# One frequency per 128x32 matmul tile in the mixing stage of a two-layer spectral kernel

## Chip, core and metric

The kernel runs on one core of a Trainium2 chip. The time is the device time of one execution in microseconds; a median of three runs is given for the kernel before.

A core has four engines that matter here: PE (TensorE: matmuls, with a weight load of its own, PEld), DVE (VectorE), ACT (ScalarE) and POOL (GpSimd). SP only issues DMAs. Matmuls write PSUM, which DVE and ACT copy out to SBUF; DMAs go between SBUF and the HBM.

## What is computed

The input is 16 images (B) of 16 channels (C), 256 x 256. Layer 0 is a 3x3 circular convolution of the group-normalized input, layer 1 a Laplace layer; each adds its result to its input. In layer 1 every frequency of the transformed image has a 16 x 16 complex matrix of its own:

```python
    x = x + _L0_conv_ref(_gn(x), L0_conv_weight)
    x = x + _L1_conv_ref(_gn(x), ...)
    # in _L1_conv_ref:
    alpha = jnp.fft.fft2(x, axes=(-2, -1))
    A = 1.0 / (omega1[:, None, None, None] - weights_pole1[None])
    Bm = 1.0 / (omega2[:, None, None, None] - weights_pole2[None])
    S = jnp.einsum('ikpq,oikp,xikq->oxik', weights_residue, A, Bm)
    output_residue1 = jnp.einsum('biox,oxik->bkox', alpha, S)
    x1 = jnp.fft.ifft2(output_residue1, s=(Ny, Nx), axes=(-2, -1)).real
```

A second term, x2, comes from the poles alone (exponentials in y and x). The change touches `output_residue1`, the product over the channels i at each frequency, which the kernel calls mixing.

## The kernel before

There are three stages, one after the other. The first convolves, normalizes and makes the forward transform; it leaves the spectrum in the HBM array `aD` (128 rows of x frequencies, 32 rows of real and imaginary channels, 256 y frequencies by 16 images). The second, the mixing, reads `aD` and writes `yD`. The third reads `yD`, transforms back, adds the transient and the input and writes the output.

The mixing stage (lines 994 to 1284) works through 32 rounds of `g` (L1242). A round handles four x frequencies (`s`): the 128 rows of a matmul are 4 x 32, real and imaginary channels. A round has four places `n` (L1250), and a place 64 of the 256 y frequencies. For each place:

- `sums` (L1036) makes on PE the weights of the next round, in PSUM banks `ps_s`, for two places at a time (at even n). Four banks hold two places.
- `spread` (L1060) copies them into the weights' tile `sg`, half by ACT (L1066) and half by DVE as a shuffle (L1069), in two steps (`odds`), which stand before the first and the second mix of the place.
- `mix` (L1132) multiplies: weights from `sg`, the moving operand from `abd[jq]`, in which each s has its own rows and all others are zero, so that the four x frequencies come out in separate columns. Four PSUM banks `ps_mix` take turns.
- the copy (L1265) brings `ps_mix` to the tile `yt`, on ACT or DVE by `m`; `late` gives one more copy to DVE in the steps in which ACT has Exp or Sin to do.
- `store` (L1153) writes `yt` to `yD`, and `load` (L1115) fetches the spectrum of the next round into the same `abd[jq]`; so that load waits for the last mix of the place. Places 0 and 1 share one tile (`pair`) and are loaded together at n = 1, before that place's store; at the other places the store comes first. All these DMAs are issued by SP, in the order in which they stand.
- steps of `weights` (small DVE and POOL work for a later round) and of `make_exps` (L1182: POOL and ACT work for the third stage) are drawn in, one a place.

Before the change two neighbouring frequencies are taken by one matmul. `sg` holds them side by side (`m e`: channel, then even or odd), so that weights of 64 columns serve both; the moving operand has 128 columns, both frequencies times 4 x 16. Each output of 64 rows by 128 columns has the products of each frequency with each spectrum, and half of them (even with odd) is of no use; the copy takes it along and the store picks the useful rows (`yt[e::2, e]`), in two DMAs. The output's upper and lower 64 rows (`t`) take two matmuls of different frequencies. A place has four mixes of eight such matmuls.

After round 30 `unmix_first` (L1160) puts one row of `yD` right: it reads it into the free `sg` tile, works on it on DVE and writes it back.

In the third stage `load_images` (L1315) fetches the first channel's spectra in pieces, as the stage starts, and `load_quarter` (L1337) fetches a later channel's in four DMAs, each ahead of its use. `combine` on POOL, `along_x` and `along_y` on PE follow. `pitched` (L62) lays out `aD` and `yD` with 256 floats between rows and 1024 at the end of a partition's part.

Of the kernel before, what the change touches and what calls it, by code (L numbers as in the profile page):

```python
# [9 lines left out]
FP = mybir.dt.float32  # L10
# [6 lines left out]
B = 16  # L17
C = 16
N = 256
# [5 lines left out]
def conv_then_laplace_kernel(ctx: ExitStack, tc: tile.TileContext, a: dict, out: bass.AP):  # L25
# [44 lines left out]
        t = dp.tile([P, C, 8 * N + 256], FP, name=f"vD{b}", tag=f"vD{b}")  # L70
        vD.append(t[:, :, 0 : 8 * N].rearrange("p c (b h x) -> p c b h x", b=4, h=2))
    aD = pitched("aD", 2 * C, N * B)
    yD = pitched("yD", 4 * C, N * B // 2, 2, 4)
    cD = dp.tile([P, 4, 8, N], FP, name="cD", tag="cD")
    hD = dp.tile([7, 2, 16, C * C * 4], FP, name="hD", tag="hD")
    eD = [dp.tile([n, P, C, 2, P], FP, name=f"eD{n}", tag=f"eD{n}") for n in (2, 1)]
# [570 lines left out]
    def chain(*gens):  # L647
        for gen in gens:
            yield from gen
# [100 lines left out]
    def pool(stage, name, bufs=1, **kw):  # L750
        return stage.enter_context(tc.tile_pool(name=name, bufs=bufs, reuse_waits="tile", **kw))
# [242 lines left out]
    ptab.close()  # L994


    yp = pool(p2, "yt", 3)
    g0 = pool(p2, "sg0")
    a0 = pool(p2, "abd0")
    wp = pool(p2, "w", 2)  # L1000
# [7 lines left out]
    pm = pool(p2, "p_mix", 4, space=PSUM)  # L1008

    def new_sg(g):  # L1010
        return (g0, g1)[g % 2].tile([P, P, 2 * C, 2], FP, name="sg", tag="sg")

# [37 lines left out]
    swap = [p ^ 4 for p in range(32)]  # L1052

    def couples(z):
        return z.rearrange("p q (n e) -> p n q e", e=2)

    def columns_of(to, k):
        return to[:, :, k : k + 2] if len(to.shape) == 4 else to[:, k : k + 2]

    def spread(n, *pairs, odds=(0, 1)):  # L1060

# [9 lines left out]
    def first_sums():  # L1071

        nc.gpsimd.memset(pair, 0.0)
        wt, w128 = (at_once(steps) for steps in first_weights)
        load(0, 1)
        nc.gpsimd.memset(abd[2], 0.0)
        load(0, 2)
        nc.sync.dma_start(  # L1080
            out=aD[16:P, 2 * C - 2 : 2 * C], in_=spec[16:P].rearrange("p r f b -> p r (f b)")
        )
        nc.gpsimd.tensor_tensor(accs, proj[:, :, :, :, 0], proj[:, :, :, :, 1], ALU.add)
        sg = new_sg(0)
        other = up["u"].tile([P, 2, 2 * C], FP, name="other", tag="other")
        for h, w in enumerate((wt, w128)):
            for n in range(4):
                fy = slice(P * h, P * h + P)
                ps = sums(n, w)
                spread(  # L1090
                    n,
                    (sg[:, 64 * h : 64 * h + 64], [couples(z[:, :, fy]) for z in ps]),
                    (other[:, 1 - h], [z[:, :, P * (1 - h)] for z in ps]),
                )
        for h in range(2):
            o, d = sg[:, 64 * h, :, 0], other[:, h]
            nc.vector.tensor_tensor(d, d, o, ALU.subtract)
            nc.vector.scalar_tensor_tensor(o, d, fixrow, o, ALU.mult, ALU.add)
        return sg
# [29 lines left out]
                    out=abd[jq][s::4, s].rearrange("r c j b -> r c (j b)"), in_=src[:, :, jq]  # L1129
                )  # L1130

    def mix(n, sg, yt):  # L1132


        ps = pm.tile([P, 4, 2, 4, B], FP, name="ps_mix", tag="ps_mix")
        jq = n // 4
        for j in range(4):
            cc, jj = divmod(4 * (n % 4) + j, 8)
            for t in range(2):
                f = 128 * t + 64 * cc + 16 * jq + 2 * jj  # L1140
                nc.tensor.matmul(  # L1141
                    ps[64 * t : 64 * t + 64, j],
                    lhsT=sg[:, f // 2].rearrange("p m e -> p (m e)"),
                    rhs=abd[jq][:, :, 2 * t + cc, 2 * jj : 2 * jj + 2].rearrange(
                        "p s j b -> p j s b"
                    ),
                    start=True,
                    stop=True,
                )
        j0 = 4 * (n % 4)  # L1150
        return yt[:, :, :, j0 : j0 + 4], ps.rearrange("p j o s b -> p o (s b) j")

    def store(g, jq, yt):  # L1153
        for e in range(2):
            nc.sync.dma_start(
                out=yD[4 * g : 4 * g + 4, :, e, jq].rearrange("s k n -> k s n"),
                in_=yt[e::2, e].rearrange("p (s b) j -> p s (b j)", s=4),
            )

    def unmix_first():  # L1160

        z2 = new_sg(32).rearrange("p (a n) m e -> p a (n m e)", a=4)[:, 0:2]
        z, t = (z2[:, j, 0:1024].rearrange("p (c n) -> p c n", c=4) for j in range(2))
        at = yD[0]
        for c in range(4):
            nc.sync.dma_start(out=z[:, c], in_=at[32 * (c // 2) : 32 * (c // 2) + 32, c % 2])
        yield
        lo, hi = z[:, 0:2], z[:, 2:4]  # L1170
        nc.vector.scalar_tensor_tensor(t[:, 0:2], hi, osgn, lo, ALU.mult, ALU.add)
        nc.vector.scalar_tensor_tensor(t[:, 2:4], lo, nosgn, hi, ALU.mult, ALU.add)
        nc.vector.tensor_scalar(t, t, 0.5, None, ALU.mult)
        t0, z0 = t[:, 0:3:2, 0:256:16], z[:, 0:3:2, 0:256:16]
        nc.vector.tensor_tensor(z0, z0, t0, ALU.subtract)
        nc.vector.scalar_tensor_tensor(t0, z0, first, t0, ALU.mult, ALU.add)
        for c in range(4):
            nc.sync.dma_start(out=at[32 * (c // 2) : 32 * (c // 2) + 32, c % 2], in_=t[:, c])

    def make_exps(which):  # L1182
# [12 lines left out]
        for q in range(8):  # L1195
            th = ep.tile([P, 2, N], FP, name="s_th", tag="s_th")
            rn = ep.tile([P, N], FP, name="s_rn", tag="s_rn")
            tmp = ep.tile([P, N], FP, name="s_tmp", tag="s_tmp")
            ex = ep.tile([P, 2, N], FP, name="s_ex", tag="s_ex")
            for j in range(2):  # L1200
                i = 2 * q + j
                nc.gpsimd.tensor_scalar(th[:, j], t, pim[:, i : i + 1], None, ALU.mult)
            magic = 1.5 * 2.0**23
            c1 = 6.28125
            c2 = float(np.float32(1.93500518798828125e-3))
            c3 = 2 * np.pi - c1 - c2
            for j in range(2):
                z = th[:, j]
                nc.gpsimd.tensor_scalar(rn, z, 1.0 / (2 * PI), turns, ALU.mult, ALU.add)
                nc.gpsimd.tensor_scalar(rn, rn, magic, magic, ALU.add, ALU.subtract)  # L1210
                for c in (c1, c2, c3):
                    nc.gpsimd.tensor_scalar(tmp, rn, float(c), None, ALU.mult)
                    nc.gpsimd.tensor_tensor(z, z, tmp, ALU.subtract)
                yield
            nc.gpsimd.tensor_scalar(th, th, most, least, ALU.min, ALU.max)
            for j in range(2):
                i = 2 * q + j
                nc.scalar.activation(ex[:, j], t, AF.Exp, scale=pl[:, i, 0:1])
            yield True
            yield  # L1220
            nc.scalar.activation(th, th, AF.Sin, bias=phase)
            yield True
            nc.gpsimd.tensor_tensor(th, th, ex, ALU.mult)
            for op, eo in ((ALU.add, 0), (ALU.subtract, 1)):
                nc.gpsimd.tensor_tensor(
                    ex[:, :, eo * P : eo * P + P], th[:, :, 0:P], th[:, :, N - 1 : P - 1 : -1], op
                )
            yield
            for o in range(2 - which):
                nc.sync.dma_start(  # L1230
                    out=eD[which][o, :, 2 * q : 2 * q + 2].rearrange("p i e t -> p i (e t)"),
                    in_=ex,
                )
            yield
# [3 lines left out]
    ahead, wt = first_sums(), None  # L1238
    o2 = finish_projections()
    unmix = None  # L1240
    exps, late = chain(make_exps(0), make_exps(1)), None
    for g in range(32):  # L1242
        sg, w_now = ahead, wt
        if g == 0:
# [5 lines left out]
        for n in range(4):  # L1250
# [6 lines left out]
            elif sets and n % 2 == 0:  # L1257
                banks = {j: sums(j, w_now) for j in (n, n + 1)}
            evict = [banks[j] for j in sets]
            yt = yp.tile([P, 2, 4 * B, 16], FP, name="yt", tag="yt")  # L1260
            for m in range(4):
                for j, ps in zip(sets, evict) if m < 2 else ():
                    spread(j, (ahead, [couples(z) for z in ps]), odds=(m,))
                o, src = mix(4 * n + m, sg, yt)
                (nc.vector.tensor_copy if m >= (2 if late else 3) else nc.scalar.copy)(o, src)  # L1265
            if n == 1 and g < 31:
                load(g + 1, n)
            store(g, n, yt)
# [6 lines left out]
            if n == 3:  # L1275
                steps = weights(g + 3) if g < 29 else iter(())
            wt = next_step(steps, None) or wt
            late = g and next(exps, None)
        if g == 30:
            unmix = unmix_first()  # L1280
            next(unmix)
# [33 lines left out]
    def load_images(yk, b0, rows, eng):  # L1315

        at = slice(16 * b0, 16 * b0 + 64)
        for r in range(2):
            for h in range(2):
                eng.dma_start(  # L1320
                    out=yk[r][rows, h].rearrange("p c b j -> p c (b j)")[:, :, at],
                    in_=yD[rows, 2 * C * h + C * r].rearrange("p e q n -> p (e q) n")[:, :, at],
                )

    def load_tables(k, eng=nc.gpsimd):
# [11 lines left out]
    def load_quarter(k, n, yk):  # L1337
        r, h = divmod(n, 2)
        nc.sync.dma_start(
            out=yk[r][:, h].rearrange("p c b j -> p (c b j)"),  # L1340
            in_=yD[:, 2 * C * h + C * r + at(k)].rearrange("p e q n -> p (e q n)"),
        )

    def load_v(k, b0):
# [305 lines left out]
```

## Time and profile before

| | |
|---|---|
| median of 3 runs | 2562.41 us (2560.56 to 2570.66) |
| the profiled execution | 2559.74 us, span 2557.7 us |
| mixing stage | about 1206 to 1794 us |
| a round of the mixing stage | 18.05 us |
| DMA in that stage | 0.77 of 16 engines, 248 GB/s |
| third stage | about 1794 to 2557 us |

The page gives for every engine its busy time, as a share of the span and in 40 slices, and then groups of instructions by line, engine, operation and form: `128*64 128x128` is a tile of the array of 128 rows by 64 columns with 128 moving columns, x its count, followed by busy time, mean ns of one, and the idle time ahead of it with what ended it. An fp32 matmul stands there as two weight loads and two matmul records. The other views ask the trace for a stretch of time: busy time of each engine, instructions in order, DMA packets.

### The profile page before, as it was taken

Reading aid. Unit: us, or ns where it says so; the run is one execution under the profiler, and the core shown is the slowest. Engines: PE = TensorE matmul, PEld = TensorE weight load, DVE = VectorE, ACT = ScalarE, POOL = GpSimd, SP = SyncE. Lnnn points to the kernel's source line nnn. Section 1 sums busy time; section 2 is a strip of 40 time slices with the busy share of each in tenths; the row PEclk is TensorE's granted clock in tenths of the full one; section 3 lists DMA queues with packets and bytes.
Section 4 is the critical chain, followed back from the end, with each engine's and each line's share of the span. In section 5 each row is a group of like instructions: output and inputs, shape, how many; then the busy total and the mean of one; then the engine's idle time right before and its main releaser. Section 6 shows DMA issues by size and latency. Waiting matters only on the chain. (4 is left out here: it accounts for less than half of the span.)

```text
span 2557.7 us, 83730 instructions
## 1 busy us (share of the span) xinstructions
PE 2446.8 (96%) x35314; PEld 1895.7 (74%) x35314; DVE 1836.5 (72%) x3771; ACT 1433.9 (56%) x2603; POOL 1255.0 (49%) x1277
## 2 busy tenths in 40 slices
PE   4999999999999999998999999999899999999998
PEld 2454555457777777775899999998688888888887
DVE  7777789848888888887566666665367676666766
ACT  2566666675666666665677767776344434444443
POOL 1333369442333333334376756664655655556553
PEclk9999999999999999999999999999899999999999
DMA  7889878865456456456777777777988888889884
GB/s 272 271 292 300 280 264 292 289 239 201 189 224 247 194 218 247 194 219 216 230 255 248 255 253 246 243 244 247 278 286 292 293 291 283 294 282 306 282 290 167
DMA packets 314070, 653.11 MB, mean 255 GB/s; under 512 B 45238, under 2 KB 160054, under 8 KB 301792
## 3 DMA queue, kind: packets, MB, share of 16 engines
q1 hardware_dynamic: 312720, 644.23, 73.2%
q8 instruction: 278, 4.55, 0.7%
q0 software_dynamic: 928, 3.02, 0.5%
q10 hardware_dynamic: 48, 0.52, 0.2%
q14 instruction: 96, 0.79, 0.1%
HBM read 368.15 MB, written 280.36 MB: 254 GB/s over the span
## 5 line engine op out<-in xcount | busy, mean ns | idle before, releaser
L1362 POOL TENSOR_TENSOR u<-yk 128x512 f32<-128x512 f32 (+1 forms) x268 | 351.7, 1345 | 313.8 <-PE ps_p L1398 243.9
L300 PE MATMUL ps_conv<-xt,wc 32*32 32x512 f32 x12288 | 447.2, 606 | 30.5 <-issue 21.0
L1141 PEld LDWEIGHTS ps_mix<-abd,sg 128*64 128x64 f32 x8192 | 446.8, 137 | 36.7 <-issue 30.0
L1141 PE MATMUL ps_mix<-abd,sg 128*64 128x128 f32 x8192 | 463.4, 274 | 9.2 <-DVE yt L1265 4.9
L300 PEld LDWEIGHTS ps_conv<-xt,wc 32*32 32x32 f32 x12288 | 252.3, 104 | 212.5 <-issue 117.7
L802 ACT ACTIVATE t<-ps_y,vmr 128x384 f32<-128x384 f32 x512 | 296.8, 580 | 156.6 <-PE ps_y L794 156.4
L786 PE MATMUL ps_y<-tabE,vq 128*128 128x256 f32 x1024 | 313.3, 388 | 1.8 <-ACT t L802 1.8
L794 PE MATMUL ps_y<-tabO,vq 128*128 128x256 f32 x1024 | 305.9, 380 | 0.0
L1422 PE MATMUL ps_f<-pt,inv 128*128 128x256 f32 x1008 | 300.5, 380 | 0.0
L1423 PE MATMUL ps_f<-hs,ey 128*128 128x256 f32 x1008 | 299.8, 379 | 0.0
L271 POOL TENSOR_TENSOR pair<-pair,far 128x1024 f32<-128x1024 f32 x64 | 151.7, 2370 | 297.2 <-DVE pair L268 195.5
L1398 PEld LDWEIGHTS ps_p<-inv,u 128*128 128x128 f32 x2048 | 268.6, 193 | 35.3 <-POOL u L1366 11.4
L1398 PE MATMUL ps_p<-inv,u 128*128 128x128 f32 x2048 | 276.2, 278 | 9.9 <-POOL u L1366 9.8
L1426 DVE TENSOR_TENSOR r<-ps_f,q 128x256 f32<-128x256 f32 x256 | 106.9, 418 | 245.0 <-ACT q L1425 224.1
L1265 ACT COPY yt<-ps_mix 128x512 f32<-128x512 f32 x352 | 203.2, 586 | 110.6 <-PE ps_mix L1141 39.4
L1425 ACT COPY q<-ps_f 128x256 f32<-128x256 f32 x256 | 95.4, 372 | 273.9 <-PE ps_f L1423 250.4
L786 PEld LDWEIGHTS ps_y<-tabE,vq 128*128 128x128 f32 x1024 | 189.5, 191 | 78.6 <-ACT q L842 50.3
L1265 DVE COPY yt<-ps_mix 128x512 f32<-128x512 f32 x160 | 108.9, 688 | 180.8 <-PE ps_mix L1141 175.4
L1400 ACT COPY pt<-ps_p 128x512 f32<-128x512 f32 x256 | 151.5, 592 | 137.1 <-PE ps_p L1398 137.1
L666 POOL TENSOR_TENSOR vq<-vf 128x512 f32<-128x512 f32 x63 | 80.1, 1272 | 289.8 <-DVE vf L670 278.8
L1066 ACT ACTIVATE sg<-ps_s,mcol 128x512 f32<-128x512 f32 (+1 forms) x264 | 178.5, 677 | 68.8 <-PE ps_s L1043 30.0
L794 PEld LDWEIGHTS ps_y<-tabO,vq 128*128 128x128 f32 x1024 | 195.5, 191 | 26.8
(243 smaller groups left out, 4037.0 us busy)
## 6 DMA issues: line engine op xcount, KB each, us to landing
xt<-in_x SPq DMA_DIRECT2D x288, 258.0 KB
vD<-pair SPq DMA_DIRECT2D x256, 256.0 KB
yD<-yt SPq DMA_DIRECT2D x256, 256.0 KB
vl<-vD SPq DMA_DIRECT2D x128, 512.0 KB
out_y<-ol SPq DMA_DIRECT2D x128, 512.0 KB
s<-vD SPq DMA_DIRECT2D x124, 512.0 KB
aD<-spec SPq DMA_DIRECT2D x15, 4096.0 KB
yk<-yD SPq DMA_DIRECT2D x60, 1024.0 KB
```

What stands on the lines that cost most here:

```text
L271: nc.gpsimd.tensor_tensor(lo, lo, hi, ALU.subtract)
L300: nc.tensor.matmul(acc[r][32 * c : 32 * c + 32], lhsT=ready[b][0][rows, phase, tap], rhs=halves[b][u // 2][rows, q : q + 5 : 4, 2 - tap : ...
L786: nc.tensor.matmul(ps[:, 0:N], lhsT=vf[:, xo, 0, j], rhs=tabE[:, 0 : i + 2 : i + 1], start=True, stop=False, skip_group_check=True,)
L794: nc.tensor.matmul(ps[:, P : P + N], lhsT=vf[:, xo, 1, j], rhs=tabO[:, i : C + 1 : C - i], start=False, stop=True, skip_group_check=True,)
L802: nc.scalar.activation(t[:, xo, j].rearrange("p l n -> p (l n)"), ps[:, 0:384], AF.Copy, scale=vmr[:, 0, b0 + j, i : i + 1],)
L1066: nc.scalar.activation(columns_of(to, k), src[odd], AF.Copy, scale=nsgn)
L1141: nc.tensor.matmul(ps[64 * t : 64 * t + 64, j], lhsT=sg[:, f // 2].rearrange("p m e -> p (m e)"), rhs=abd[jq][:, :, 2 * t + cc, 2 * jj : 2 ...
L1265: (nc.vector.tensor_copy if m >= (2 if late else 3) else nc.scalar.copy)(o, src)
L1362: nc.gpsimd.tensor_tensor(u[:, :, j].rearrange("p b (c n) -> p c b n", c=8), in0, in1, o)
L1398: nc.tensor.matmul(ps[:, at], lhsT=u[:, n], rhs=tab, start=True, stop=True)
L1422: nc.tensor.matmul(ps[:, e], lhsT=tab, rhs=pt[:, e], start=True, stop=False)
L1423: nc.tensor.matmul(ps[:, e], lhsT=ey[:, e], rhs=hs, start=False, stop=True)
```

## The change

Each mixing matmul takes one frequency. The array is cut into four tiles of 128 rows by 32 columns (`c` = 2t + e), each with the 32 weights of one frequency, and the moving operand is that frequency's 64 columns. Nothing in the output is left over, so a PSUM bank holds eight values of j instead of four, and a place has two mixes (`m` = `cc`) of 8 x 4 matmuls in place of four mixes of 4 x 2. `sg` keeps a frequency's 32 channels in one run; `spread` writes into that order. `yt` is half as large, and there are six of it instead of three. A place's results go out in one DMA over 128 partitions. `yD` has 8 x 16 = 128 rows of 1024 floats (plus 256) instead of 64 of 2048 (plus 256). The flag `late` is gone: the first mix's copy is ACT's, the second's DVE's. In the third stage `load_images` has eight DMAs where it had four, and a quarter's load takes two runs of 1024 floats from each partition instead of one of 2048.

```diff
-    yD = pitched("yD", 4 * C, N * B // 2, 2, 4)
+    yD = pitched("yD", 8 * C, N * B // 4, 1, 4)[:, :, 0]
...
-    yp = pool(p2, "yt", 3)
+    yp = pool(p2, "yt", 6)
...
     def new_sg(g):
-        return (g0, g1)[g % 2].tile([P, P, 2 * C, 2], FP, name="sg", tag="sg")
+        return (g0, g1)[g % 2].tile([P, N, 2 * C], FP, name="sg", tag="sg")
...
     def couples(z):
-        return z.rearrange("p q (n e) -> p n q e", e=2)
+        return z.rearrange("p q n -> p n q")
...
-    def mix(n, sg, yt):
-        ps = pm.tile([P, 4, 2, 4, B], FP, name="ps_mix", tag="ps_mix")
-        jq = n // 4
-        for j in range(4):
-            cc, jj = divmod(4 * (n % 4) + j, 8)
-            for t in range(2):
-                f = 128 * t + 64 * cc + 16 * jq + 2 * jj
+    def mix(n, cc, sg, yt):
+        ps = pm.tile([P, 8, 4, B], FP, name="ps_mix", tag="ps_mix")
+        for j in range(8):
+            for c in range(4):
+                t, e = divmod(c, 2)
                 nc.tensor.matmul(
-                    ps[64 * t : 64 * t + 64, j],
-                    lhsT=sg[:, f // 2].rearrange("p m e -> p (m e)"),
-                    rhs=abd[jq][:, :, 2 * t + cc, 2 * jj : 2 * jj + 2].rearrange(
-                        "p s j b -> p j s b"
-                    ),
+                    ps[32 * c : 32 * c + 32, j],
+                    lhsT=sg[:, 128 * t + 64 * cc + 16 * n + 2 * j + e],
+                    rhs=abd[n][:, :, 2 * t + cc, 2 * j + e],
                     start=True,
                     stop=True,
                 )
-        j0 = 4 * (n % 4)
-        return yt[:, :, :, j0 : j0 + 4], ps.rearrange("p j o s b -> p o (s b) j")
+        return yt[:, :, 8 * cc : 8 * cc + 8], ps.rearrange("p j s b -> p (s b) j")

     def store(g, jq, yt):
-        for e in range(2):
-            nc.sync.dma_start(
-                out=yD[4 * g : 4 * g + 4, :, e, jq].rearrange("s k n -> k s n"),
-                in_=yt[e::2, e].rearrange("p (s b) j -> p s (b j)", s=4),
-            )
+        nc.sync.dma_start(
+            out=yD[4 * g : 4 * g + 4, :, jq].rearrange("s k n -> k s n"),
+            in_=yt.rearrange("p (s b) j -> p s (b j)", s=4),
+        )
...
-            yt = yp.tile([P, 2, 4 * B, 16], FP, name="yt", tag="yt")
-            for m in range(4):
-                for j, ps in zip(sets, evict) if m < 2 else ():
+            yt = yp.tile([P, 4 * B, 16], FP, name="yt", tag="yt")
+            for m in range(2):
+                for j, ps in zip(sets, evict):
                     spread(j, (ahead, [couples(z) for z in ps]), odds=(m,))
-                o, src = mix(4 * n + m, sg, yt)
-                (nc.vector.tensor_copy if m >= (2 if late else 3) else nc.scalar.copy)(o, src)
+                o, src = mix(n, m, sg, yt)
+                (nc.vector.tensor_copy if m else nc.scalar.copy)(o, src)
...
         for r in range(2):
-            for h in range(2):
+            for c in range(4):
+                h, e = divmod(c, 2)
                 eng.dma_start(
-                    out=yk[r][rows, h].rearrange("p c b j -> p c (b j)")[:, :, at],
-                    in_=yD[rows, 2 * C * h + C * r].rearrange("p e q n -> p (e q) n")[:, :, at],
+                    out=yk[r][rows, h, 4 * e : 4 * e + 4].rearrange("p c b j -> p c (b j)")[:, :, at],
+                    in_=yD[rows, 2 * C * c + C * r][:, :, at],
                 )
...
         nc.sync.dma_start(
-            out=yk[r][:, h].rearrange("p c b j -> p (c b j)"),
-            in_=yD[:, 2 * C * h + C * r + at(k)].rearrange("p e q n -> p (e q n)"),
+            out=yk[r][:, h].rearrange("p (e c) b j -> p e (c b j)", e=2),
+            in_=yD[:, 4 * C * h + C * r + at(k) :: 2 * C][:, 0:2].rearrange("p e q n -> p e (q n)"),
         )
```

## The prediction

> **What bounds the kernel now.** I read the page first: the span, the busy shares, the 40 slices. PE is busy 96% of the span, and in every slice but the first, so each stage has to be asked what its PE time is made of.
>
> ```profile
> span 2557.7 us, 83730 instructions
> PE 2446.8 (96%) x35314; PEld 1895.7 (74%) x35314; DVE 1836.5 (72%) x3771; ACT 1433.9 (56%) x2603; POOL 1255.0 (49%) x1277
> ...
> L1141 PEld LDWEIGHTS ps_mix<-abd,sg 128*64 128x64 f32 x8192 | 446.8, 137 | 36.7 <-issue 30.0
> L1141 PE MATMUL ps_mix<-abd,sg 128*64 128x128 f32 x8192 | 463.4, 274 | 9.2 <-DVE yt L1265 4.9
> ...
> L1265 ACT COPY yt<-ps_mix 128x512 f32<-128x512 f32 x352 | 203.2, 586 | 110.6 <-PE ps_mix L1141 39.4
> ...
> L1265 DVE COPY yt<-ps_mix 128x512 f32<-128x512 f32 x160 | 108.9, 688 | 180.8 <-PE ps_mix L1141 175.4
> ```
>
> The copies out of PSUM wait for the mixing matmuls; these wait for next to nothing. The tile view of ps_mix puts the stage at 1206 to 1794 us, 32 rounds of g. Next the table by stretches, with two rounds in mid-stage:
>
> ```profile
> core 0: us, PE busy (x) PEld busy (x) DVE busy (x) ACT busy (x) POOL busy (x), PEclk, DMA share, GB/s
> 1502.88:1520.93 18.05, 18.05 (x387) 16.29 (x385) 10.60 (x28) 11.49 (x20) 5.76 (x7) 1.00 0.81 265
> ...
> 1575.08:1593.13 18.05, 18.05 (x387) 16.29 (x385) 11.39 (x29) 12.64 (x21) 9.93 (x11) 1.00 0.79 249
> ```
>
> A round lasts 18.05 us with PE busy throughout and the others at 10 to 12.6; but the DMA engines are busy 0.8 of it, and they are second in line. The timeline of one half round shows the two parts of PE's work, and the DMA view the cost of packets over 25 rounds (1250 to 1701.25):
>
> ```profile
> 1502.88 1.96 PE L1043 MATMUL ps_s<-ct,w 64*32 64x256 f32 x64
> ...
> 1504.76 7.21 PE L1141 MATMUL ps_mix<-abd,sg 128*64 128x128 f32 x128
> ...
> 1511.90 1.96 PE L1043 MATMUL ps_s<-ct,w 64*32 64x256 f32 x64
> ```
>
> ```profile
> DMA packets 101252, 112.17 MB, mean 249 GB/s; under 512 B 8510, under 2 KB 85670, under 8 KB 101158
> ## 3 DMA queue, kind: packets, MB, share of 16 engines
> q1 hardware_dynamic: 101158, 110.78, 76.1%
> ```
>
> Half a round is 1.88 us of ps_s and 7.14 us of mixing: 128 records (each fp32 matmul leaves two), so 55.8 ns a record. Two 128*64 tiles run side by side, so a tile takes a 128-column record every 111 ns. The DMA: 0.761 x 16 x 451.25 us / 101158 packets = 54 ns a packet of mostly 1 KB; 112.17 MB / 25 = 4.49 MB a round; all queues together hold 77.3% (76.1 + 1.1 + 0.1) of the time, so a round needs 0.773 x 18.05 = 13.95 us of 16 busy engines.
>
> **What the skill says.** "TensorEngine Tiling (Array Packing)", Performance Considerations, promises up to 4x for column tiling, but warns of some 60 cycles a matmul (so do not shrink a dimension that is small already) and of PSUM evacuation as the next bottleneck. "TensorE: Matmul & The Clock Gate", Back-to-back issue gap, gives N/2.4 + 2.5 ns a matmul of N columns, with a floor near 25 ns. The trace agrees with the slope if a record passes each column twice: 2 x 128/2.4 + 2.5 = 109 ns against 111. It does not bear the floor out where several tiles work: 60 records of ps_h on 32*32 tiles took 1.43 us in the chain (24 ns, 256 columns each), and they started about 7 ns apart in a burst and 17 ns later. "DMA: Bandwidth & Descriptors", Rules for kernel authors, advises one 128-partition transfer instead of two halves, since both share the same 16 engines: so I take no bandwidth from the single store.
>
> **The change, part by part.**
> (1) Matmuls. Before, a round issues 128 matmuls = 256 records, 128 columns on two tiles; half of each output is thrown away. After: 8 x 4 x 8 = 256 matmuls = 512 records, 64 columns on four tiles. A 128*32 tile stands in the trace already: psd. Its 16 records take 0.66 us with one of 0.273 us to drain, so (0.66 - 0.273)/15 = 26 ns a record, 103 ns a tile for 128 columns, as on 128*64: narrowing costs nothing and four tiles do run side by side. For 64 columns no row exists. From below, half of it: 2 x 64/2.4 + 2.5 = 56 ns a tile, 14 ns a record. From above, no gain from the halved columns: 26 ns. I take 14, because the slope fits 128 and 256 columns (256: 2 x 256/2.4 + 2.5 = 216; ps_s on eight tiles 1.88 us / 64 x 8 = 235 with its drain). A 32-column weight load (psd's 110 ns against 137) overlaps, as now. PE's round: 512 x 14 = 7.2, plus 2 x 1.88 of ps_s, plus some 0.3 of drains: **11.2 us** (17.2 from above).
> (2) Copies. 16 per round become 8, each still 128x512. ACT loses 11 - 4 = 7 x 0.586 = 4.1 us a round, DVE 5 - 4 = 1 x 0.688 = 0.7. ACT goes to some 8, DVE to some 10.5: not the bound. The flag that moved a copy to DVE in the steps with Exp and Sin goes: ACT's table load and two Exps (1.28 + 2 x 0.50) now stand in front of ACT's copy and of the next sums' eviction. PE's slack under the DMA bound (about 3 us) covers that; without it, 2.3 us twice in seven steps is 1.1 steps x 2.3 = 2.6 us a round.
> (3) Spreads: the same 512 elements, runs of two words rather than four on the write, and a strided PSUM read. Unseen; the mix copies already read PSUM with a long stride at 586 ns, so nothing. From above, 0.1 us on each of 8 a round on either engine, under cover.
> (4) SP. Stores fall from 8 to 4 a round, with twice the rows each. An issue now takes about 0.6 us. Bounds 0.6 to 1.25 us: SP's round is 12 loads x 0.65 + 4 x (0.6 to 1.25) = 10.2 to 12.8 us. The load of abd for the next round stands behind the store of the place before (except at n = 1), which waits for both copies; SP thus stays below the DMA bound, but not by much.
> (5) DMA. Same 1 KB rows, same bytes. More instructions: 512 more a round, two 16 KB blocks, about 0.1 us. So **14.0 us a round** at full share: as PE falls to 11.2, this becomes the bound. The abd tiles are single: their load starts when the last mix of the place has ended. At 1493.96 us the four loads of a pair were issued (2.56 us), and the last packet came some 6.2 us after the first issue; between that point and the next use lie 3.8 of ps_s and 4 x 64 x 14 ns = 1.8 x 2 of mixing, some 7.4 us. Tight, but behind it the stores and other loads keep the queue filled. A full queue is not quite reached: the slices of the page that move most stand at 0.9. I take 0.94: 13.95/0.94 = **14.8 us**, or 303 GB/s, which is the page's best slice (306).
> (6) The last stage. A quarter's load takes 2 x 4 KB rows for one of 8 KB; it is issued more than one unit (11.5 us, a quarter of the 46 us between like entries of the chain) ahead, and PE is 99% busy there (595.62 of 600 us from 1900 on), so nothing. At the seam the first images need 8 POOL DMAs for 4; 4 took 3.71 us, with half the rows each they take less: about +1.9 us (0 to 3.7), on the path, since PE waits there for yk.
>
> **The sum.** Rounds 1 to 29: 29 x (18.05 - 14.8) = 94. Round 0 is held until 1219 us by DMA of the stage before and then by the load of abd[3]: its last mixes shorten by 1.5. Round 30 (15.96 us, no sums) falls to about 14: 2. Round 31 stalls at unmix's read of yD (PE idle about 5 us): 1. Seam: -1.9. Together 97 us. The profiled execution took 2559.7 (span 2557.7): 2463. The median of runs is 2.7 higher: 2465.
>
> **Rivals.** A, the forecast: DMA bound at 0.9 to 1.0 share, rounds of 14.0 to 15.6: 2440 to 2490. B, DMA packets get quicker than the mean shows, since some of their time is other traffic: rounds of 12 to 13.9, near PE's 11.2: 2385 to 2440. For it: a packet's time includes its waiting beside others, and the stage never had to move more than it did. Against: 12.5 us would be 359 GB/s, and no slice of the page passes 306. C, the chain takes over: 64-column records cost up to 26 ns, or ACT's Exp steps and SP's order hold the next pair's load back; rounds of 15.7 to 17.4: 2490 to 2540. D, slower: yD's rows now lie 5 KB apart instead of 9 KB. If that makes the HBM writes dearer, the stage is DMA bound and pays at once: 2048 store packets a round, so 10 ns on each is 1.28 us a round. The DMA needs (18.05 - 14.0)/1.28 x 10 = 32 ns more, 54 to 86, before the round is longer than now; at 100 ns it is 19.9 us, 2562 + 31 x 1.85 = 2620. For it: DMA is second in line already. Against: the 54 ns are a mean over stores of yD and loads of aD, whose rows lie 17 KB apart, and nothing in it points to the stride. E, the change does not do what it says: four tiles queue up one behind the other. Then 56 ns a record and 512 x 56 = 28.7 us a round: about 2970; psd speaks against it.
>
> **Chances.** A 0.58, B 0.12, C 0.15, D 0.08, E 0.03, and 0.04 for a balance at no change. A measurement tells about 0.5% (13 us). Faster 0.85, same 0.04, slower 0.11. The range takes in most of B and nearly all of C: 2415 to 2545.
>
> **What would show it.** Step 1: 16384 records of ps_mix on 128*32, about 14 to 17 ns apart, and a round's PE below 12 us of work. Step 2: 128 copies on each engine. Step 5: a round near 14.8 us with DMA share above 0.9, idle PE before ps_mix put down to abd. It is wrong if PE is again busy through the round, if the share stays near 0.8, or if 1 KB packets cost much over 54 ns.

## The result and the profile after

The changed kernel takes 2673.66 us in the median (2666.8 to 2679.11, 5 runs), against 2561.17 us for the kernel before (2555.77 to 2570.66, 5 runs): ratio 1.0433, 95% interval 1.0403 to 1.0463. It is slower, where 2465 us were forecast. The profiled execution took 2679.11 us.

These lines of the page of the kernel after answer to those of before (in a group: out and in, count, busy us and mean ns, then idle time of the engine ahead of it and what ended it):

```profile
span 2677.3 us, 99892 instructions
PE 2333.6 (87%) x43506; PEld 1734.0 (65%) x43506; DVE 1961.0 (73%) x3739; ACT 1329.0 (50%) x2379; POOL 1260.6 (47%) x1281
...
PE   5899999989999999986666666666699999999998
...
DMA  7788888755566556646666766666898888888884
...
L1139 PE MATMUL ps_mix<-abd,sg 128*32 128x64 f32 x16384 | 310.4, 237 | 213.9 <-issue 212.0
...
L1139 PEld LDWEIGHTS ps_mix<-abd,sg 128*32 128x32 f32 x16384 | 279.5, 122 | 262.8 <-issue 259.7
...
L1069 DVE STREAM_SHUFFLE sg<-ps_s 128x512 f32<-128x512 f32 (+1 forms) x264 | 327.9, 1326 | 0.0
...
L1259 DVE COPY yt<-ps_mix 128x512 f32<-128x512 f32 x128 | 89.3, 698 | 182.8 <-PE ps_mix L1139 182.7
```

In the mixing stage, now 1208 to 1916 us, PE is busy for 0.67 of the time and the DMA engines for 0.65 (the table by stretches below). Neither is full, so the stage is not bound as before (PE) nor as forecast (DMA). The mixing matmuls have 213.9 us of idle PE ahead of them, and 212.0 of it ends in "issue": PE waited for nothing that the profile shows. It does not stand under `abd`, as the prediction had it for its DMA bound. The copies then wait for those matmuls. A second row has changed: the shuffle of `spread` takes 1326 ns in the mean, mostly one form. The last stage has not: it lasts 761 us (1916 to 2677), before it was 764.

The table by stretches, over the same 400 us of the mixing stage, first of the kernel before, then after (busy us and number of instructions of each engine, clock, DMA share, GB/s):

```profile
1300.00:1700.00 400.00, 400.00 (x8500) 360.81 (x8498) 257.56 (x646) 288.08 (x481) 260.82 (x289) 1.00 0.78 250
```

```profile
1300.00:1700.00 400.00, 267.62 (x11745) 209.64 (x11741) 284.49 (x513) 177.46 (x269) 212.04 (x237) 0.90 0.65 207
```

Matmuls and weight loads together are 16998 before and 23486 after, so 42.5 and 58.7 instructions a microsecond on PE ("a us" from here on). A round of before has 768 of them (256 + 128 matmul records and as many loads), one of after 1280 (512 + 128, and as many loads). 1280 at 58.7 a us are 21.8 us: that is the new round (22.0 in the mean over rounds, 18.7 to 25.0). The DMA view of the kernel after has the instructions as a queue of their own:

```profile
q1 hardware_dynamic: 72961, 81.31, 63.8%
q8 instruction: 93, 1.52, 1.6%
```

93 packets for 23486 instructions are one of 16 KB for 253. The timeline of a round, of which only PE's lines with a pause ahead of them and their neighbours are shown (start, duration, instructions taken together, and in brackets the idle time before):

```profile
1573.22 1.99 PE L1139 MATMUL ps_mix<-abd,sg 128*32 128x64 f32 x128 [0.99 <-issue]
...
1576.97 1.25 PE L1139 MATMUL ps_mix<-abd,sg 128*32 128x64 f32 x73 [1.75 <-issue]
...
1578.14 2.25 PE L1043 MATMUL ps_s<-ct,w 64*32 64x256 f32 x53
...
1582.33 1.09 PE L1043 MATMUL ps_s<-ct,w 64*32 64x256 f32 x11 [1.94 <-issue]
...
1583.36 2.89 PE L1139 MATMUL ps_mix<-abd,sg 128*32 128x64 f32 x116
...
1588.48 3.49 PE L1139 MATMUL ps_mix<-abd,sg 128*32 128x64 f32 x127 [2.23 <-issue]
...
1592.43 0.42 PE L1139 MATMUL ps_mix<-abd,sg 128*32 128x64 f32 x13 [0.46 <-issue]
```

Count the matmul records from one pause to the next: 128, then 73 + 53, then 11 + 116, then 127. With their weight loads that is 256, 252, 254, 254 instructions: PE runs through one 16 KB block and stops. Within a block the matmuls run as forecast: 128 records in 1.99 us, less 0.22 for the last one's drain, are 14 ns each. The packet records of the instruction queue put the starts of the blocks at 1574.57, 1579.91, 1586.24 and 1589.84 us; PE went on 2.2 to 2.6 us after each. From 1330 to 1700 us there are 70 pauses of over 0.7 us, against 86 blocks; from the start of one instruction to the start of the next they are 2.0 us long in the mean. Counted with the sequencer's own instructions among them (waits and the like, under 3 a block), 61 of the 69 distances between pauses are one or two blocks of 256, within 4. In the median a block's packet starts only 0.7 us before PE stops; PE goes on 2.4 us after that start, and 1.4 us after the packet has ended.

### The profile page after: what moved, and what is told of

The parts are those of the page before. It is cut to its first block, busy times and chain, and to the rows that moved or that the text cites. A ratio compares the mean times of both kernels' runs of the same rounds, so it can differ in the third digit from the quotient of the medians.

```text
span 2677.3 us, 99892 instructions
## 1 busy us (share of the span) xinstructions
PE 2333.6 (87%) x43506; PEld 1734.0 (65%) x43506; DVE 1961.0 (73%) x3739; ACT 1329.0 (50%) x2379; POOL 1260.6 (47%) x1281
## 4 chain that ended last, share of the span: by engine, by line
PE 77%; issue 10%; DVE 8%; DMA 2%; POOL 1%; ACT 1%; SPq 1%; DVEq 0%; ACTq 0%; POOLq 0%
PE ps_conv L300 14%; PE ps_mix L1139 10%; PE ps_y L786 9%; PE ps_y L794 8%; PE ps_p L1394 7%; PE ps_f L1418 7%; PE ps_f L1419 7%; PE ps_s L1043 6%; PE ps_x L829 4%; PE ps_h L1378 2%; PE psd L814 1%; DVE r L1427 1%; DVE ol L1429 1%; DVE ol L1430 1%; PE ps_setup L494 1%
## 5 line engine op out<-in xcount | busy, mean ns | idle before, releaser
L1358 POOL TENSOR_TENSOR u<-yk 128x512 f32<-128x512 f32 (+1 forms) x268 | 357.2, 1366 | 309.9 <-PE ps_p L1394 249.1
L1139 PE MATMUL ps_mix<-abd,sg 128*32 128x64 f32 x16384 | 310.4, 237 | 213.9 <-issue 212.0
L1139 PEld LDWEIGHTS ps_mix<-abd,sg 128*32 128x32 f32 x16384 | 279.5, 122 | 262.8 <-issue 259.7
L1069 DVE STREAM_SHUFFLE sg<-ps_s 128x512 f32<-128x512 f32 (+1 forms) x264 | 327.9, 1326 | 0.0
L1259 DVE COPY yt<-ps_mix 128x512 f32<-128x512 f32 x128 | 89.3, 698 | 182.8 <-PE ps_mix L1139 182.7
```

Of the source, the lines that this page charges most:

```text
L1069: nc.vector.stream_shuffle(columns_of(to, C + k), src[1 - odd], swap)
L1139: nc.tensor.matmul(ps[32 * c : 32 * c + 32, j], lhsT=sg[:, 128 * t + 64 * cc + 16 * n + 2 * j + e], rhs=abd[n][:, :, 2 * t + cc, 2 * j + e ...
L1358: nc.gpsimd.tensor_tensor(u[:, :, j].rearrange("p b (c n) -> p c b n", c=8), in0, in1, o)
```

## The experiments

The theory, called F: PE gets its instructions no faster than some 59 a us in this stage, because each block is fetched late; 1280 a round make the round. The first rivals: the shuffle, now nearly twice as long, holds PE's weights back (theory S); or narrow matmuls and four tiles cost more than their records show (theory T). Runs e1 to e7 are single runs beside a run of before on the same chip (2564.83 us for e1 to e4, 2559.32 for e5 to e7). "Round" is the mean distance of like records of `ps_mix` over the stage.

**e1, more instructions and nothing else.** The kernel before, with each mixing matmul cut into two of 64 columns: tiles, weights, copies, shuffles and stores as before.

```diff
-                nc.tensor.matmul(
-                    ps[64 * t : 64 * t + 64, j],
-                    lhsT=sg[:, f // 2].rearrange("p m e -> p (m e)"),
-                    rhs=abd[jq][:, :, 2 * t + cc, 2 * jj : 2 * jj + 2].rearrange(
-                        "p s j b -> p j s b"
-                    ),
+                for o in range(2):
+                    nc.tensor.matmul(
+                        ps[64 * t : 64 * t + 64, j, o],
+                        lhsT=sg[:, f // 2].rearrange("p m e -> p (m e)"),
+                        rhs=abd[jq][:, :, 2 * t + cc, 2 * jj + o],
...
```

> The kernel before, with each mixing matmul cut into its two halves of 64 columns with the same weights: the same products in twice as many instructions (1280 PE instructions a round in place of 768), the same tiles, layout, copies and stores. Theory F (instructions reach PE no faster than some 60 a us, 256 about every 4.2 us): rounds of 21 to 22.5 us, time 2650 to 2700. Theory S (the slower shuffle on DVE is what lengthens the round): the shuffle stays at 0.73 us here, rounds of 18.1 to 19 us, 2560 to 2590. Theory T (the narrow tiles are the cause): as S.

**e2, half of the mixing instructions.** The kernel after, with one matmul of 128 columns for two frequencies that stand two apart, both with the weights of the first. Columns through PE, copies, shuffles and DMAs are those of after.

```diff
-        for j in range(8):
+        for j in range(0, 8, 2):
...
+                at = 2 * j + e
...
-                    ps[32 * c : 32 * c + 32, j],
+                    ps[32 * c : 32 * c + 32, j : j + 2],
...
-                    rhs=abd[n][:, :, 2 * t + cc, 2 * j + e],
+                    rhs=abd[n][:, :, 2 * t + cc, at : at + 3 : 2].rearrange("p s j b -> p j s b"),
```

> The kernel after, with one matmul of 128 columns for two frequencies of like parity (the weights of the first are used for both, so the second one's products are not the reference's): the same 128*32 tiles, the same column time, half the matmuls, 768 PE instructions a round. F: PE no longer starves; the next bound is DVE with the shuffle at 1.35 us (15.4 us a round) or DMA (14 to 15): rounds of 15 to 16.5, 2460 to 2510. S: nothing changes for DVE, rounds stay at 21 to 22 us, 2650 to 2680. T: the same, 2650 to 2680.

**e3, the shuffle's old layout.** The kernel after, with `sg` in the order of before (even and odd frequency side by side), so that the weights of a matmul are read with a stride of two words.

```diff
-        return (g0, g1)[g % 2].tile([P, N, 2 * C], FP, name="sg", tag="sg")
+        return (g0, g1)[g % 2].tile([P, P, 2 * C, 2], FP, name="sg", tag="sg")
...
-        return z.rearrange("p q n -> p n q")
+        return z.rearrange("p q (n e) -> p n q e", e=2)
...
-                    lhsT=sg[:, 128 * t + 64 * cc + 16 * n + 2 * j + e],
+                    lhsT=sg[:, 64 * t + 32 * cc + 8 * n + j, :, e],
```

> The kernel after, with the weights' tile in the order of before (two frequencies side by side, a matmul takes every second column); all else as after. Shuffle back to 0.73 us. F: rounds stay at 21 to 22.4 us, 2640 to 2680. S: rounds fall to 15 to 17 us, 2460 to 2530. T: no change, 2660 to 2680.

**e4, both.** The edits of e2 and e3 together.

> Both of these edits on the kernel after (half the instructions, the order of before for the weights; every second frequency is given its neighbour's weights). F and S together: nothing is left but DMA and PE, rounds of 14 to 15.5 us with DMA share above 0.9, 2440 to 2480, as the prediction had it for its bound. T: no change, 2650 to 2680. If it stands well above 2480, a third cause is at work.

What these four measured:

| run | us | round, us | PE instructions a round | a us | DMA share | shuffle, us |
|---|---|---|---|---|---|---|
| before | 2561.17 | 18.06 | 768 | 43 | 0.78 | 0.73 |
| after | 2673.66 | 21.96 | 1280 | 59 | 0.65 | 1.35 |
| e1 | 2677.03 | 21.72 | 1280 | 59 | 0.67 | 0.73 |
| e2 | 2521.36 | 16.85 | 768 | 46 | 0.83 | 1.35 |
| e3 | 2666.56 | 21.77 | 1280 | 59 | 0.66 | 0.73 |
| e4 | 2496.89 | 15.89 | 768 | 49 | 0.89 | 0.73 |

Three kernels with 1280 instructions a round, one of them with the tiles, the copies and the weights' order of before, have the same round within 1.2%; the kernels with 768 have whatever round their other work gives. The count of instructions decides, and neither the tiles nor the layout. The pauses say the same: in e3 all 71 distances between pauses of over 0.7 us are one or two blocks; in e1, where a block keeps PE busy for longer, the pauses are shorter (34 of over 0.5 us, 0.96 us in the mean), and all 33 distances are whole blocks. Nor is it the clock granted to PE, which was 0.90 in after (the third number from the end in the table by stretches) and 1.00 in e1. In the table by stretches of e1, and below it of e3, PE is called busy for 373 and 259 us, but the instructions executed in 400 us are the same to 0.6%:

```profile
1300.00:1700.00 400.00, 372.99 (x11864) 333.95 (x11856) 217.56 (x542) 241.68 (x400) 208.94 (x234) 1.00 0.67 210
```

```profile
1300.00:1700.00 400.00, 259.03 (x11796) 203.49 (x11788) 206.31 (x520) 175.57 (x272) 207.78 (x232) 0.92 0.66 210
```

The shuffle is back at 0.73 us in e3, and the run stands 7 us under the median of after, at the lower end of the runs of after (2666.8), so no gain can be told from the spread. Where fewer instructions are asked for it counts: e4 is 24 us under e2. These are single runs, and executions of after alone spread over 12 us, so the size is rough; the rounds (16.85 and 15.89 us) agree. In e2 DVE had become the busiest engine, and in e4 (second) it has room and the DMA share rises to 0.89:

```profile
1300.00:1700.00 400.00, 311.15 (x9124) 242.08 (x9128) 357.85 (x664) 225.05 (x348) 279.33 (x311) 0.94 0.83 265
```

```profile
1300.00:1700.00 400.00, 325.15 (x9757) 251.87 (x9752) 280.98 (x706) 238.54 (x375) 295.67 (x328) 0.96 0.89 284
```

Both e2 and e4 stayed above what was expected of them (by 11 and 17 us). In e4 PE still waits for "issue", at only 49 instructions a us:

```profile
PEld ps_mix L1140 <- issue: 66.8, 81, 6.1
...
PE ps_mix L1140 <- issue: 31.6, 28, 2.7
```

The mean hides the dense parts: its mixing matmuls, 256 records of 28 ns with as many loads, ask for 512 instructions in 7.2 us, 71 a us. But of the 49 distances between its pauses of over 0.7 us only 18 are whole blocks, so the fetch is only a part of this. How much of e4's round is the fetch, how much other waits and how much the DMA engines' last tenth was not separated.

**e5, is it the DMA traffic that delays the blocks?** The kernel after, without the loads of spectra for rounds 2 to 31.

```diff
-            if n == 1 and g < 31:
+            if n == 1 and g < 1:
                 load(g + 1, n)
...
-            if n != 1 and g < 31:
+            if n != 1 and g < 1:
                 load(g + 1, n)
```

> The kernel after without the loads of the spectrum for rounds 2 to 31 (they mix the spectrum of round 1 again, so the products are not the reference's). PE's instructions, the copies and the stores are unchanged; DMA moves half. If instructions come late because their 16 KB blocks queue among the data's packets (F1), the rate rises clearly over 59 a us: rounds of 15.5 to 19 us, 2470 to 2580. If the supply has its own pace (F2), 59 a us and rounds of 21 to 22 us stay: 2640 to 2680. If the waits were for abd after all, PE's waits vanish and rounds fall to DVE's 15 to 16 us: 2460 to 2500, with rates above 75 a us.

2622.21 us, rounds of 20.03, between what F1 and F2 expected:

```profile
1300.00:1700.00 400.00, 277.06 (x12809) 211.37 (x12798) 309.48 (x560) 194.42 (x295) 235.51 (x263) 0.94 0.35 121
```

With half the traffic gone, 25607 instructions in 400 us are 64 a us: the ceiling rises by 9% and stays. The pauses still come a block or two apart (66 of 78 distances), of 1.65 us instead of 2.0, and PE still goes on 1.4 us after a block's packet has ended. So the waits were not for `abd`, and a smaller part of the delay comes with the loads' traffic. Most of it stays with the DMA engines 0.35 busy; what makes it up is not shown.

**e6, below the ceiling.** e1, with only every second matmul (odd j) cut in two: 1024 instructions, which at 59 a us take 17.3 us, less than the 18.06 of PE's columns.

```diff
-                for o in range(2):
+                for o in (0, 1) if j % 2 else (slice(0, 2),):
...
+                        rhs=abd[jq][:, :, 2 * t + cc, 2 * jj + o]
+                        if j % 2
+                        else abd[jq][:, :, 2 * t + cc, 2 * jj : 2 * jj + 2].rearrange("p s j b -> p j s b"),
```

> The kernel before with every second mixing matmul cut into two halves of 64 columns: 1024 PE instructions a round, evenly spread, the same products. At 59 instructions a us these take 17.3 us, less than the 18.05 us of column time. F: rounds of 18.1 to 19 us, 2560 to 2595, that is hardly a loss: the supply binds only from some 1065 instructions a round. If each further matmul costs by itself (as much as in the run with all cut, half of 3.7 us): rounds of 19.9 us, some 2620.

2580.5 us; every round 18.64, as even as before, at 55 instructions a us and with as little waiting for "issue" ahead of the mixing loads (17.7 us in 400) as before (18.1). The 256 more instructions cost 0.58 us, 4.5 ns for each of 128 more matmul records, and no pause of over 0.5 us. So e1's loss is not twice this one's: 256 such records would be 1.2 us a round, and e1 lost 3.7, which leaves some 2.5 to the supply, if the two simply add. At 55 a us nothing is lost to supply where the rate is even.

**e7, what the shuffle pays for.** The kernel after, with both sides of `spread` walked in the other order: PSUM is read contiguously, and single words are written 128 bytes apart.

```diff
-        return z.rearrange("p q n -> p n q")
+        return z
...
-        return to[:, :, k : k + 2] if len(to.shape) == 3 else to[:, k : k + 2]
+        return to[:, :, k : k + 2].rearrange("p n k -> p k n") if len(to.shape) == 3 else to[:, k : k + 2]
```

> The kernel after, with the spread walking along n first and then over the two channels: reads of PSUM in one long run, writes of single words 128 B apart, in place of pairs of words written and single words read 1 KB apart. The time is held by the instruction supply in any case: 2650 to 2685. The question is the shuffle's own duration: back to 0.73 us if the scattered read made it 1.35; 1.35 or more if the short runs of the write did.

2766.72 us, far above the 2650 to 2685 expected: the supply no longer holds the time. The tile view of `sg`, 1300 to 1700 us, of after and then of e7 (durations in ns, least, median and largest):

```profile
L1069 DVE STREAM_SHUFFLE sg<-ps_s x146: 1289/1350/1472, 1301.7 to 1696.9; 128x512 f32<-128x512 f32 x146
L1066 ACT ACTIVATE sg<-ps_s,mcol x146: 678/707/764, 1303.1 to 1699.8; 128x512 f32<-128x512 f32 x146
```

```profile
L1069 DVE STREAM_SHUFFLE sg<-ps_s x131: 2433/2555/2844, 1298.4 to 1699.8; 128x512 f32<-128x512 f32 x131
...
L1066 ACT ACTIVATE sg<-ps_s,mcol x129: 1074/1126/1237, 1301.9 to 1694.1; 128x512 f32<-128x512 f32 x129
```

A shuffle of 512 words took 0.73 us with 128 written runs of four words (before, e3), 1.35 with 256 runs of two, 2.55 with 512 single words: (2.55 - 0.73)/384 = 4.7 ns for each more run. The read got simpler in e7, so there it is the write; for the first step, from before to after, read and write both changed, and what speaks for the write is the like price, 4.8 ns for each of 128 more runs. ACT, with the same pattern, pays nothing for runs of two (0.69 before, 0.71 after) and 0.4 us for single words. Here DVE became the bound:

```profile
1300.00:1700.00 400.00, 254.46 (x10382) 196.19 (x10382) 393.33 (x457) 205.35 (x236) 191.47 (x214) 0.87 0.58 185
```

**e8 to e11, the change on one place of four.** If instructions are the price, a part of the change should pay: with only the last place of a round in the new form (two lots of 32 narrow matmuls, a lot being what fills one PSUM bank, and two copies), a round has 896 instructions, 15.2 us at 59 a us, and PE's columns fall to 16.6 us. `sg` stays in the order of before, so the shuffle stays at 0.73. These four have 4 to 20 executions each.

```diff
+    def mix_one(n, cc, sg, yt):
+        ps = pm.tile([P, 8, 4, B], FP, name="ps_one", tag="ps_mix")
+        for j in range(8):
+            for c in range(4):
+                e, t = divmod(c, 2)
+                nc.tensor.matmul(
+                    ps[32 * c : 32 * c + 32, j],
+                    lhsT=sg[:, 64 * t + 32 * cc + 8 * n + j, :, e],
+                    rhs=abd[n][:, :, 2 * t + cc, 2 * j + e],
...
```

In e8 the first lot stands behind the second place's mixes and the other ahead of the third's; this place's spreads then come with no mixes beside them.

> The kernel before, with one of the four places of a round (the last) in the form of after: 64 single-frequency matmuls on 128*32 tiles, in two lots that stand between the other places' matmuls; layout, stores and third stage as before, the same products. Column time of a round 3.5 (ps_s) + 192 x 0.0546 + 128 x 0.014 + 6 changes of tiles at 0.15 = 16.6 us; 896 PE instructions, at 59 a us 15.2 us. F: the supply no longer binds and the columns do, rounds of 16.6 to 17.3 us, 2515 to 2545, faster than both kernels. If narrow tiles or the mixture of forms cost by themselves: 18 us a round or more, 2560 or more.

2664.45 us against 2562.6, ratio 1.0402 (1.0367 to 1.0437), rounds of 21.4 at 42 instructions a us: far off. The fetch is not the main cause: of the 41 distances between pauses of over 0.7 us one alone is a whole block, and the commonest are 324 and 578 instructions, which make one round: pauses stand at fixed places of the round. So the loss was looked for in the order of the work.

> As e8 (the kernel before with the last of a round's places in the single-frequency form), with this place's spreads moved to between the mixes of the place ahead of it, and its second lot of narrow matmuls behind that place's mixes, so that DVE and ACT have matmuls beside them. Instructions stay 896 a round. If e8's loss was the order of the work (spreads at the round's end with nothing on PE): PE's own 16.6 us of columns a round or the 15.2 us that 896 instructions take at 59 a us decide, with some waits left: rounds of 16.8 to 18.2 us, 2520 to 2560 us. If it is the narrow lots themselves (records that start later after a change of tile, instructions supplied in bursts) or the loads of spectra: rounds of 19 us and more, 2590 us and more.

2670.03 us against 2561.82, ratio 1.0402 (1.0367 to 1.0437): moving the spreads gained nothing. The waits of e9, 1300 to 1800 us (total, times, longest), name a load (in e8 the same wait stood at 37.9 us in 17 times):

```profile
PE ps_one L1158 <- DMA abd<-aD: 77.5, 23, 6.2
PEld ps_one L1158 <- issue: 70.3, 22, 6.4
```

The narrow lots use the spectra half a round earlier than the place did before, but its load was still issued at the round's end. In e10 it goes right behind the second lot:

```diff
+            if n == 2 and 0 < g < 31:
+                load(g + 1, 3)
             store(g, n, yt)
```

> As e9, with the loads of the last place's spectra issued directly behind the second lot of narrow matmuls, ahead of the third place's stores and loads, rather than at the end of the round. In e9 every round has PE waiting for these spectra ahead of the first narrow lot (77.5 us in 23 waits in 500 us, some 3.4 a wait, with instructions recorded as late by as much there). If these loads are what holds e9 back, the wait goes: rounds of 16.8 to 18.5 us, 2510 to 2570 us. If it is another wait (spreads, stores, lots of narrow matmuls), the loads were only the last to come and the round stays at 20.5 us or more: 2630 us and more.

2570.36 us against 2560.21, ratio 1.0035 (1.002 to 1.005), rounds of 18.2. The earlier load was worth 100 us, which confirms that wait; but the time stands at the very top of what was expected. The next waits in line are for stores (waits of e10, 1300 to 1800 us):

```profile
ACT yt L1295 <- DMA yD<-yt: 83.0, 32, 9.9
...
DVE yt L1298 <- DMA yD<-yt: 58.8, 22, 4.9
```

The last place's output buffer, one of three, is held from the first lot to its store. In e11 both lots stand behind the third place's mixes, to hold it for less time.

> As e10, with both narrow lots behind the third place's mixes (in e10 the first is behind the second place's), so that the last place's output buffer, one of three, is held for the time of the two lots and its store rather than for half a round. In e10, 142 us of 500 are copies of ACT and DVE waiting for stores to free these buffers. Instructions stay 896 a round, PE's columns 16.6 us. If that is what keeps e10 at 18.2 us a round: 16.7 to 17.7 us, 2510 to 2545 us. If stores or loads are late anyway (the round's last four DMAs crowd together): 18 us or more, 2555 to 2600 us.

2579.6 us, ratio 1.0068 (1.0047 to 1.0089): no gain, and in the range expected if stores or loads are late anyway. ACT's waits for stores fall to 46.0 us, and those of ACT and DVE for the mixing matmuls rise (from 44.1 to 67.7 and from 64.1 to 71.4). No version here beats the kernel before with every frequency at its own weights; whether a partial form can was not settled.

## Why the prediction was wrong

The step that failed is (1), "PE's round 11.2 us", together with the entry for instructions in (5): "512 more a round, two 16 KB blocks, about 0.1 us". PE's round was summed from the time of its records, and the instructions that bring them were priced as DMA bytes. The bytes are indeed next to nothing (1.6% of the DMA time), but PE waits for most of the blocks: 1280 instructions took 21.8 us, at 59 a us, where 11.2 were forecast. That term was missing, and with it a rival: those that had PE slower, E (tiles that queue up) and the first half of C (records of up to 26 ns), were about the records themselves, and these come 14 ns apart on tiles that do run side by side.

The Trainium skill, "Runtime: NRT & Kernel Launch", Instruction fetch mechanics, has what should have raised the question: PE's instructions come in blocks of 16 KiB, 256 each. This case agrees (93 packets for 23486). It also calls the fetch hidden behind the pace of issue, and a block's crossing mostly so. Here it was not: pauses of 2.0 us in the mean, 70 of them for 86 blocks.

The profile of before could have warned, though it shows no ceiling. The forecast round of 14.8 us needs 1280/14.8 = 86 instructions a us. In the convolution stage of before, the densest of six stretches of 100 us ran 2573 + 2556, 51 a us, and the densest of 5 to 20 us 61 to 66: none of 5 us or more came near 86. That stage's weight loads (32*32 tiles) also stood idle under "issue", which by itself proves nothing, since its matmuls hardly did:

```profile
L300 PE MATMUL ps_conv<-xt,wc 32*32 32x512 f32 x12288 | 447.2, 606 | 30.5 <-issue 21.0
...
L300 PEld LDWEIGHTS ps_conv<-xt,wc 32*32 32x32 f32 x12288 | 252.3, 104 | 212.5 <-issue 117.7
```

Point by point:

- (1) Records 14 ns apart on four tiles: right, 14 ns within a block. The 11.2 us of work are there, by this spacing, spread over 22 us.
- (2) Copies: right, 128 for each engine; they are not the bound.
- (3) Spreads, "so nothing. From above, 0.1 us on each": mis-sized. DVE's eight a round take 1.35 us each for 0.73, 5 us more a round, since the write runs of two words count and not the words. In this kernel no cost of it can be told (e3); with 768 instructions a round it costs some 24 us (e4 against e2). "Unseen" was said of it, and the upper bound was then taken from a copy that writes in another way.
- (4) SP and its order: not the bound in after. Between e9 and e10 the place of a load on SP was worth 100 us, so the care was due.
- (5) DMA bound at a share of 0.94 and 14.8 us: never reached, since PE is late. e4, with 768 instructions and the old shuffle, came to 0.89 and 15.9 us, 2497 us, some 30 us above the forecast; since PE still has waits there, it does not show whether a share of 0.94 can be had.
- (6) Last stage: right, nothing lost.
- D, dearer stores at the new pitch: false. The mean time of a 1 KB packet (loads and stores together, 1300 to 1700 us) is 50.1 ns after, 49.6 before.

Taken away in this order, the gap of 209 us splits thus: 152 us between after and e2 are instructions, 24 us between e2 and e4 the shuffle, and 32 us between e4 and the forecast were not separated: a DMA queue that isn't quite full and what waits PE still has.

## What to carry to other kernels

Count the instructions that a stage puts on PE, matmuls and weight loads (an fp32 matmul makes four), and divide by the time it is to take: no run here held more than 59 a us over 400 us of the mixing stage with its loads and stores running, whatever the records' own durations say. Smaller tiles and fewer columns raise the rate that is asked for at the same work, so they can pay only where columns are the bound and the rate has room. When a profile says "issue" on PE, count the instructions between pauses: 256 or a multiple of it was the fetch here, while pauses at fixed places of a round (e8) were another wait.

## What the runs showed of the hardware

- PE's instructions: a ceiling of 59 a us with the DMA engines 0.65 to 0.67 busy, and 64 with 0.35; pauses of 2.0 and 1.65 us in the mean, mostly 256 or 512 instructions apart; 55 a us ran without pauses (e6). Why a block isn't asked for earlier stays open.
- The shuffle on DVE took longer with shorter written runs: 0.73, 1.35, 2.55 us for the same 512 words in runs of 16, 8 and 4 bytes. An activation on ACT in the same patterns took 0.69, 0.71, 1.13.
- Four 128*32 tiles take a 64-column fp32 record every 14 ns in all, within a block.
